# A mixture-of-experts routing stage: weights multiplied by ScalarE, smaller one-hot chunks, experts counted on partitions, and gathers recorded in order

## The chip, the cores and the metric

The kernel runs on one NeuronCore of a Trainium2 chip. Its engines work side by side, each through its own list of instructions in order: PE (TensorE, matrix products; PEld is its weight load), DVE (VectorE), ACT (ScalarE), POOL (GpSimd, which also issues the indirect DMAs) and SP (SyncE, which issues the plain DMAs). They wait for each other through semaphores. SBUF is the working memory, with 128 partitions; PSUM takes what PE computes. The metric is the device time of one execution in microseconds, the median of several runs. All data are float32.

## The reference, cut to what matters

The input is one image of 256 channels and 48x48 pixels, which is 2304 tokens of 256 numbers. Three blocks follow, each added to the stream:

- group norm and an attention of 4 heads in which the 2304 x 4 head rows all attend to each other (9216 queries, 9216 keys);
- layer norm and a "slice" attention: 64 slices, tokens assigned softly by a softmax `sw`, attention among slice tokens, and back to the tokens with the same weights;
- layer norm and a mixture of eight experts.

The last one is where the change lies:

```python
gate_logits = xf @ Wg + bg
top_w, top_i = jax.lax.top_k(gate_logits, TOP_K)      # TOP_K = 2
top_w = jax.nn.softmax(top_w, axis=-1)
w_dense = jnp.sum(jax.nn.one_hot(top_i, E) * top_w[..., None], axis=1)
for e in range(E):                                     # E = 8
    h = jax.nn.gelu(xf @ W1[e] + b1[e], approximate=False)
    out = out + w_dense[:, e:e + 1] * (h @ W2[e] + b2[e])
```

Only two of the eight experts of a token have a weight other than zero, so the kernel computes only those.

## The kernel before, in words

Tokens lie on the partitions in 18 tiles of 128 (`NTT = 18`, `P = 128`). The kernel is one function, `layers`, with five stages in time. First come the loads and projections, then the first attention, which runs from 67 to about 1239 us and is not touched. Then follow three short stages that the change does touch, and the mixture of experts itself. At the end `to_columns` turns the result back to channels and writes it out. A second call of `layers` stands behind a condition for extreme inputs and is not executed here.

**Who sets the order.** The program is written for a tile framework whose scheduler may reorder instructions within an engine's list. Four wrappers made from the class `InOrder` (line 49), called `pe`, `dve`, `act` and `pool`, pin each instruction behind the one recorded just before it on the same engine. Work recorded through `nc.tensor`, `nc.gpsimd` and so on is left to the scheduler. A pinned instruction stays behind its predecessor, but the scheduler may still move an instruction recorded later, without a pin, ahead of both. Since the wrapper issues every wrapped instruction, the profile gives all of them line 57; they are told apart by the names of their tiles. DMAs on SP (`nc.sync`) are not wrapped.

**Back to tokens and layer norm (lines 857 to 905).** For each of the 18 tiles PE makes `py` = the slice attention's output. DVE adds it to the stream `t_sb` for even tiles. For odd tiles PE itself adds `t_sb` through a product with the identity `ident`, and ACT copies the sum out to `t_sb`. DVE takes mean and variance (`bn_stats`, `bn_aggr`), POOL makes 1/sqrt (`rstd_t`) and the negative product with the mean (`shift`). Tiles go in groups of 6, 6, 4 and 2. After each group SP writes the rows of `t_sb` to memory (`t_d`), and the function `normed` lets ACT compute the normalised rows `tn2` (shown by the profile as `tn`) of the group before, one `ACTIVATE` per tile, which SP writes to `tn_d` in memory. There are two `tn2` buffers, so the third group's waits until the first group's write is done.

**Gating and slots (lines 913 to 999).** DVE computes the logits `lg` from what the slice attention already left in the last eight columns of `t_sb`, subtracts the mean part, multiplies by `rstd_t`, and finds the first and the second maximum of each token (`first_max`). ACT computes `e2`, the exponential of their difference; then it loads its table for gelu. Each expert's tokens are put into whole tiles of 128 rows, called slots. There can be at most `NSL` = 43 slots and at least `SURE` = 36. Products with a triangular and a full matrix of ones (`pin`, `pto`) count tokens before each token; two scans make from these the position of each of the 2 x 18 (choice, tile) pairs' tokens: `first_slot` (which slot) and `row` (which row in it).

**One-hot products (lines 1000 to 1055).** For every one of the K = 36 pairs, `in_tile` is 1 in the column of the slot that the token of this partition goes to, and `in_row` is 1 in the column of the row (it is written over the memory of `t_sb`). `what` is `in_tile` times two numbers per token, the token's index plus one and its gate weight (`wk`, flattened `wkf`). The sum over the 36 pairs of the products `in_row`^T `what` on PE gives in PSUM (`pw`) for each slot and row the token (`slot_t`) and its weight (`slot_w`). DVE builds these in chunks of G = 9 pairs: one multiply for `what` (9 x 2 x 43 = 774 elements), one comparison for `in_row` (9 x 128 = 1152), and `in_tile` in two parts of 18 pairs (774). Between the first two chunks `find_experts` counts on one partition, from the running sums `ends`, which expert each slot belongs to (`expert_i`) and how many slots are used (`used_i`). The function `busy` records products whose result is not used: 7 ahead of the one-hot products and 14 behind them, all into a PSUM tile called `spin`.

**The experts (lines 1057 to 1195).** For each slot `rows` (line 1081) gathers 128 rows of `tn_d` by `slot_t` with an indirect DMA of POOL into `xs` (two buffers, and seven separate ones, `late_xs`, for the slots after the 36th). `load_w1` loads the expert's first weights, 1 MB, by SP. `turn` transposes `xs` on PE, `first` makes the hidden layer with 16 products and eight gelus, `second` makes 8 products with the second weights, in the middle of which the next slot's `turn` is recorded. DVE adds the bias and multiplies by `slot_w`, and POOL adds the rows to `t_d` by an indirect DMA (line 1142). In this data 39 slots are used. The gathers and the adding DMAs are issued through `nc.gpsimd`, without a pin: in the list of POOL's instructions the seven late gathers stand third to ninth, and slot 2's gather tenth.

Of the kernel before, what the change touches and what calls it, by code (L numbers as in the profile page):

```python
# [9 lines left out]
FP = mybir.dt.float32  # L10
# [5 lines left out]
P = 128  # L16
# [14 lines left out]
E = 8  # L31
# [31 lines left out]
def layers(  # L63
# [666 lines left out]
    with tc.tile_pool(name="sa", bufs=1) as sa:  # L730
# [126 lines left out]
        def normed(i0, n):  # L857

            tn2 = norm.tile([P, 6, C], FP, name="tn2", tag="tn2")
            for i in range(i0, i0 + n):  # L860
                act.activation(
                    tn2[:, i - i0, :], t_sb[:, i, 0:C], AF.Identity,
                    bias=shift[:, i : i + 1], scale=rstd_t[:, i : i + 1],
                )
            nc.sync.dma_start(
                out=tn_d[i0 * P : (i0 + n) * P, :].rearrange("(i p) c -> p i c", p=P),
                in_=tn2[:, 0:n, :],
            )

        shift = const.tile([P, NTT], FP, name="shift")  # L870
        with tc.tile_pool(name="ps_y0", bufs=7, space=PSUM) as ps_y0, tc.tile_pool(
            name="norm", bufs=2
        ) as norm:
            groups = [(0, 6), (6, 6), (12, 4), (16, 2)]
            for g, (i0, n) in enumerate(groups):
                pys = [ps_y0.tile([P, C + E], FP, name="py", tag="py") for _ in range(n)]
                for k, py in enumerate(pys):
                    j, u = divmod(i0 + k, 2)
                    rows = slice(u * S, (u + 1) * S)
                    pe.matmul(py, swT[rows, j, :], tw[rows, :], start=True, stop=(u == 0))  # L880
                for k in range(1, n, 2):
                    pe.matmul(pys[k], ident, t_sb[:, i0 + k, :], start=False, stop=True)
                for k, py in enumerate(pys):
                    i = i0 + k
                    s6 = small.tile([P, 6], FP, name="s6", tag="s6")
                    if k % 2 == 0:
                        dve.tensor_tensor(t_sb[:, i, :], t_sb[:, i, :], py, ALU.add)
                        dve.bn_stats(s6, t_sb[:, i, 0:C])
                    else:
                        dve.bn_stats(s6, py[:, 0:C])  # L890
                        act.copy(t_sb[:, i, :], py)
                    dve.bn_aggr(stats[:, i, :], s6)
                these = slice(i0, i0 + n)
                ve = small.tile([P, n], FP, name="ve6", tag="ve6")
                dve.tensor_scalar(ve, stats[:, these, 1], 1e-5, None, ALU.add)
                pool.tensor_tensor(rstd_t[:, these], ve, mhalf[:, 0:n], ALU.pow)
                pool.tensor_tensor(shift[:, these], stats[:, these, 0], rstd_t[:, these], ALU.mult)
                pool.tensor_scalar(shift[:, these], shift[:, these], -1.0, None, ALU.mult)
                nc.sync.dma_start(
                    out=t_d[i0 * P : (i0 + n) * P, :].rearrange("(i p) c -> p i c", p=P),  # L900
                    in_=t_sb[:, these, 0:C],
                )
                if g > 0:
                    normed(*groups[g - 1])
            normed(*groups[-1])


    used_i = route.tile([1, 1], mybir.dt.int32, name="used_i")
# [5 lines left out]
    with gating, tc.tile_pool(name="onehot", bufs=1) as oh, tc.tile_pool(  # L914
# [82 lines left out]
        row = gp.tile([P, K], FP, name="row")  # L997
        dve.scalar_tensor_tensor(row, first_slot, -BIG, slot, ALU.add, ALU.subtract)
        in_tile = oh.tile([P, K, NSL], FP, name="in_tile")
        what_flat = oh.tile([P, K * 2 * NSL], FP, name="what")  # L1000
        what = what_flat.rearrange("p (k w n) -> p k w n", k=K, w=2)
        in_row = t_flat[:, 0 : K * P].rearrange("p (k r) -> p k r", r=P)
        pwide = ps_lg.tile([P, P], FP, name="pw")
        pw = pwide[:, 0 : 2 * NSL].rearrange("p (w n) -> p w n", w=2)
        busy(7, spin)
        G = 9
        wkf = wk.rearrange("p k i w -> p (k i) w")

        def find_tile(k, n):
# [2 lines left out]
                in_tile[:, ks, :], bc(first_slot[:, ks], [P, n, NSL]),  # L1012
                at_big.unsqueeze(1).to_broadcast([P, n, NSL]), ALU.is_equal,
            )

        past = gp.tile([1, NSL, E - 1], FP, name="past")

        def find_experts():

            dve.tensor_tensor(  # L1020
                past, bc(steps[0:1, 0:NSL], [1, NSL, E - 1]),
                ends[0:1, 0 : E - 1].unsqueeze(1).to_broadcast([1, NSL, E - 1]), ALU.is_ge,
            )
            ex = gp.tile([1, NSL], FP, name="ex")
            dve.tensor_reduce(ex, past, AX.X, ALU.add)
            dve.tensor_copy(expert_i, ex)
            dve.tensor_copy(used_i, ends[0:1, E - 1 : E])

        for k in range(0, K, G):
            ks = slice(k, k + G)  # L1030
            if k % NTT == 0:
                find_tile(k, NTT)
            dve.tensor_tensor(
                what[:, ks], in_tile[:, ks, :].unsqueeze(2).to_broadcast([P, G, 2, NSL]),
                wkf[:, ks, :].unsqueeze(3).to_broadcast([P, G, 2, NSL]), ALU.mult,
            )
            dve.tensor_tensor(
                in_row[:, ks, :], bc(row[:, ks], [P, G, P]),
                back.unsqueeze(1).to_broadcast([P, G, P]), ALU.is_equal,
            )  # L1040
            if k == 0:
                find_experts()
        for j in range(K):
            n = 2 * NSL if j % G == G - 1 else P
            pe.matmul(
                pwide[:, 0:n], in_row[:, j, :], what_flat[:, j * 2 * NSL : j * 2 * NSL + n],
                start=(j == 0), stop=(j == K - 1),
            )
        busy(14, spin)

        empties = gp.tile([P, NSL], FP, name="empties")
        dve.tensor_scalar(empties, pw[:, 0, :], 0.0, spare, ALU.is_equal, ALU.mult)
# [11 lines left out]
    with tc.tile_pool(name="ps_h", bufs=1, space=PSUM) as ps_h, tc.tile_pool(  # L1064
# [14 lines left out]
        late_xs = iter([fp.tile([P, C], FP, name=f"late_xs{s}") for s in range(SURE, NSL)])  # L1079

        def rows(s, xs):
            nc.gpsimd.indirect_dma_start(  # L1082
                out=xs, out_offset=None, in_=tn_d[:, :],
                in_offset=bass.IndirectOffsetOnAxis(ap=slot_t[:, s : s + 1], axis=0),
                bounds_check=NT + P - 1, oob_is_err=True,
            )
            return xs
# [36 lines left out]
        def second(s, hid, meanwhile):  # L1124

            e = expert_of(s, mybir.EngineType.PE)
            py = next(ring_py)
            for f in range(NHC):
                pe.matmul(
                    py, hid[:, f, :],  # L1130
                    w2_sb[:, bass.ds(e, 1), f, :].rearrange("p e d -> p (e d)"),
                    start=(f == 0), stop=(f == NHC - 1),
                )
                if f == 2:
                    meanwhile()
            e = expert_of(s, mybir.EngineType.DVE)
            y = next(ring_y)
            dve.tensor_tensor(
                y, py, b2_e[:, bass.ds(e, 1), :].rearrange("p e d -> p (e d)"), ALU.add
            )  # L1140
            dve.tensor_scalar(y, y, slot_w[:, s : s + 1], None, ALU.mult)
            nc.gpsimd.indirect_dma_start(  # L1142
                out=t_d[:, :], out_offset=bass.IndirectOffsetOnAxis(ap=slot_t[:, s : s + 1], axis=0),
                in_=y, in_offset=None, bounds_check=NT + P - 1, oob_is_err=True,
                compute_op=ALU.add,
            )
# [128 lines left out]
```

## Time and profile before

| what | us |
|---|---|
| median of 3 runs | 1622.19 (1619.83 to 1622.56) |
| the profiled execution's own time | 1621.32 |
| its span, first to last instruction | 1619.3 |
| PE busy | 1569.0 (97%), 13230 products' passes |
| DVE busy | 1046.2 (65%) |
| ACT busy | 810.8 (50%) |
| POOL busy | 140.3 (9%) |
| mean granted TensorE clock | 0.990 |

The span is made of instructions on the chip; the device time holds a little more before and after them, 2.0 us in this execution. A row of the profile's timeline gives the start in us, the duration, the engine, the source line, the operation, its output and inputs with sizes, and in brackets how long the engine had been idle before it and what ended the wait. In a table of stages each engine has its busy time and, in brackets, its number of instructions; the three last numbers of a row are the granted TensorE clock, the mean busy share of the DMA engines and GB/s. A float32 product shows as two passes of PE, each with its weight load. Durations of single instructions overlap a little where the next does not depend on the one before.

### The profile page before, as it was taken

How to read it: one execution, taken by the hardware profiler on the slowest of the kernel's cores; microseconds unless marked ns; L12 is line 12 of the kernel's file. 1: busy time of each engine (PE TensorE's matmuls, PEld its weight loads, DVE VectorE, ACT ScalarE, POOL GpSimd, SP SyncE). 2: the span in 40 equal slices, each digit the busy share in tenths (PEclk: the TensorE clock that was granted, in tenths of full speed). 3: DMA queues.
4: the chain of work that ended last, by engine and by line, in shares of the span. 5: the costliest groups of instructions: out<-in, count | busy, mean ns of one | idle time of the engine just before them, and what ended most of it. 6: DMA issues, size and time to landing. Idle time of an engine off the chain costs nothing. (4 is left out here: it accounts for less than half of the span.)

```text
span 1619.3 us, 31854 instructions
## 1 busy us (share of the span) xinstructions
PE 1569.0 (97%) x13230; PEld 786.1 (49%) x13230; DVE 1046.2 (65%) x1369; ACT 810.8 (50%) x1100; POOL 140.3 (9%) x128
## 2 busy tenths in 40 slices
PE   7999999999999999999999999999999699999995
PEld 3633343333333333333333333333335489999995
DVE  7577778777787877877878778778687721111111
ACT  2365555555555655556556555565553322333321
POOL 0000000000000000000000000000000143333321
PEclk9999999999999999999999999999999899999997
DMA  4000000000000000000000000000003756666665
GB/s 137 1 1 1 1 1 1 1 1 1 1 1 1 2 1 1 1 1 2 1 1 1 1 1 1 1 1 1 1 2 98 253 182 189 178 181 190 173 157 181
DMA packets 39910, 79.26 MB, mean 49 GB/s; under 512 B 3613, under 2 KB 26218, under 8 KB 39626
## 3 DMA queue, kind: packets, MB, share of 16 engines
q1 hardware_dynamic: 32074, 66.35, 12.3%
q0 software_dynamic: 7680, 10.75, 3.8%
q8 instruction: 108, 1.77, 0.5%
q14 instruction: 48, 0.39, 0.1%
HBM read 64.64 MB, written 12.45 MB: 48 GB/s over the span
## 5 line engine op out<-in xcount | busy, mean ns | idle before, releaser
L57 DVE TENSOR_TENSOR acc<-acc,p 128x1024 f32<-128x1024 f32 x612 | 748.2, 1222 | 251.6 <-ACT p L57 243.5
L57 ACT ACTIVATE p<-s 128x1024 f32<-128x1024 f32 x648 | 662.9, 1023 | 490.0 <-PE s L57 479.8
L57 PE MATMUL av<-p,v_sb 64*64 64x512 f32 x5184 | 675.4, 590 | 1.0 <-DVE up L57 0.7
L57 PE MATMUL s<-q,kk 64*64 64x512 f32 x5184 | 676.2, 591 | 0.0
L57 PEld LDWEIGHTS s<-q,kk 64*64 64x64 f32 x5184 | 201.6, 133 | 352.6 <-issue 181.7
L57 PEld LDWEIGHTS av<-p,v_sb 64*64 64x64 f32 x5184 | 195.6, 131 | 358.3 <-ACT p L57 202.5
L57 ACT ACTIVATE hid<-ph,bcol 128x128 f32<-128x128 f32 x312 | 89.3, 368 | 216.9 <-PE ph L57 216.2
L57 PE MATMUL py<-w_sb,hid 128*128 x624 | 147.3, 379 | 0.0
L57 PEld LDWEIGHTS ph<-xT,w 128*128 128x128 f32 x1248 | 145.3, 192 | 2.7 <-DVE xT L57 0.8
L57 PE MATMUL ph<-xT,w 128*128 128x128 f32 x1248 | 145.7, 275 | 0.5 <-DVE xT L57 0.5
L57 POOL TENSOR_TENSOR rstd_t<-ve,mhalf 128x1 f32<-128x1 f32 (+3 forms) x22 | 28.0, 1271 | 1234.1 <-DVE ve L57 1234.1
L57 DVE COPY xT<-pt 128x256 f32<-128x256 f32 x40 | 17.0, 425 | 173.3 <-PE pt L57 173.3
L57 PEld LDWEIGHTS py<-w_sb,hid 128*128 128x128 f32 x624 | 112.7, 190 | 12.2
L1142 POOL DMA_INDIRECT t_d<-y,slot_t x39 | 61.7, 1583 | 98.7 <-DVE y L57 86.2
L57 DVE TENSOR_TENSOR y<-py,b_bc 128x256 f32<-128x256 f32 x39 | 16.6, 425 | 68.6 <-PE py L57 68.6
L1082 POOL DMA_INDIRECT xs<-tn_d,slot_t x36 | 38.4, 1065 | 110.6 <-PE pt L57 83.8
L57 DVE RECIPROCAL rinv<-pb 128x256 f32<-128x256 f32 x18 | 31.5, 1751 | 0.0
L57 DVE TENSOR_TENSOR acc<-p 128x1024 f32<-128x1024 f32 x18 | 22.1, 1225 | 9.9 <-ACT p L57 9.9
L314 DVE TENSOR_SCALAR q<-pp,bcol 64x512 f32<-64x512 f32 (+1 forms) x30 | 20.8, 694 | 7.4 <-PE pp L297 7.1
L57 DVE TENSOR_REDUCE up<-av 128x512 f32<-128x1024 f32 x18 | 21.9, 1217 | 0.0
L319 ACT ACTIVATE kk<-pp,bcol 128x512 f32<-128x512 f32 (+1 forms) x10 | 6.4, 644 | 21.8 <-PE pp L301 21.8
L297 PE MATMUL pp<-t_sb,WqT 128*128 128x512 f32 (+1 forms) x40 | 17.2, 553 | 0.0
(260 smaller groups left out, 602.0 us busy)
## 6 DMA issues: line engine op xcount, KB each, us to landing
w<-in_L_ffn_W_dram SPq DMA_DIRECT2D x40, 1024.0 KB, 5.6
w_sb<-in_L_ffn_W_dram SPq DMA_DIRECT2D x8, 1024.0 KB, 13.1
x_sb<-in_x_dram SPq DMA_DIRECT2D x4, 576.0 KB
t<-t_d SPq DMA_DIRECT2D x4, 512.0 KB, 6.9
out_dram<-ob SPq DMA_DIRECT2D x4, 512.0 KB
t_d<-t_sb SPq DMA_DIRECT2D x2, 768.0 KB, 3.6
tn_d<-tn SPq DMA_DIRECT2D x2, 768.0 KB, 3.7
b_bc<-in_L_ffn_b_dram SPq DMA_DIRECT2D x1, 1024.0 KB
```

The source lines that it names most:

```text
L57: return self.tc.keep_in_program_order(getattr(self.engine, name)(*args, **kwargs))
L297: nc.tensor.matmul(pq[:, 0:tn], WqT[:, c, cols], xn[:, c, toks], start=(c == 0), stop=(c == 1))
L314: nc.vector.tensor_scalar(dst, pq[rows, 0:tn], bcol[rows, B_Q + m : B_Q + m + 1], 0.125, ALU.add, ALU.mult,)
L319: nc.scalar.activation(kk[:, m, toks], pk[:, 0:tn], AF.Identity, bias=bk_m)
L1082: nc.gpsimd.indirect_dma_start(out=xs, out_offset=None, in_=tn_d[:, :], in_offset=bass.IndirectOffsetOnAxis(ap=slot_t[:, s : s + 1], axis= ...
L1142: nc.gpsimd.indirect_dma_start(out=t_d[:, :], out_offset=bass.IndirectOffsetOnAxis(ap=slot_t[:, s : s + 1], axis=0), in_=y, in_offset=None ...
```

## The change

It has five parts.

1. In the loop over groups PE's products are recorded pair by pair: each odd tile's product with the identity follows its own first product, where before all first products of a group came first.
2. `normed` of the first group is still recorded in the second pass of the loop, those of the other three groups after the loop. In the resulting list of ACT the last copy to `t_sb` stands ahead of the second group's six `tn` activations; in the list of SP the last write to `t_d` stands ahead of that group's write to `tn_d`.
3. The one-hot tiles are built in chunks of 3, 6, 9, 9, 6 and 3 pairs; `in_tile` in parts of 9, 9 and 18. DVE multiplies only the token half of `what`; the weight half is made by ACT, one `ACTIVATE` with `AF.Copy` and a per-partition `scale` for each of the 36 pairs (43 elements). The products are recorded chunk by chunk with the tiles. `find_experts` compares on 128 partitions, one slot on each, sums over seven experts, transposes the column with PE to a row `pex`, and DVE copies this to `expert_i` ahead of the third chunk.
4. Behind the one-hot products stand 9 unused products in place of 14.
5. The gathers and the adding DMAs of the experts are issued through `pool`, with the pin. In the resulting list of POOL five late gathers stand third to seventh, slot 2's gather eighth, the two other late gathers after it; slots 3 and 4 follow as before. Elsewhere in the experts' part, PE's list differs in the first slot alone, where the third product of `second` stands ahead of the second slot's products of `first`, not behind them.

```diff
@@ back to tokens @@
                     pe.matmul(py, swT[rows, j, :], tw[rows, :], start=True, stop=(u == 0))
-                for k in range(1, n, 2):
-                    pe.matmul(pys[k], ident, t_sb[:, i0 + k, :], start=False, stop=True)
+                    if u == 1:
+                        pe.matmul(py, ident, t_sb[:, i0 + k, :], start=False, stop=True)
...
-                if g > 0:
-                    normed(*groups[g - 1])
-            normed(*groups[-1])
+                if g == 1:
+                    normed(*groups[0])
+            for group in groups[1:]:
+                normed(*group)
@@ one-hot products @@
-        what_flat = oh.tile([P, K * 2 * NSL], FP, name="what")
-        what = what_flat.rearrange("p (k w n) -> p k w n", k=K, w=2)
+        what_flat = oh.tile([P, K * 2 * NSL + P], FP, name="what")
+        what = what_flat[:, 0 : K * 2 * NSL].rearrange("p (k w n) -> p k w n", k=K, w=2)
...
             )
-
-        past = gp.tile([1, NSL, E - 1], FP, name="past")
+            for j in range(k, k + n):
+                act.activation(what[:, j, 1], in_tile[:, j, :], AF.Copy, scale=wkf[:, j, 1:2])
 
         def find_experts():
 
+            past = gp.tile([P, E - 1], FP, name="past")
+            dve.tensor_scalar(past, ends[:, 0 : E - 1], token1[:, 0:1], None, ALU.is_lt)
+            ex = gp.tile([P, 1], FP, name="ex")
+            dve.tensor_reduce(ex, past, AX.X, ALU.add)
+            pex = ps_lg.tile([1, P], FP, name="pex")
+            pe.transpose(pex, ex, ident)
+            dve.tensor_copy(used_i, ends[0:1, E - 1 : E])
+            return pex
+
+        find_tile(0, 9)
+        k = 0
+        for n in (3, 6, 9, 9, 6, 3):
+            ks = slice(k, k + n)
+            if k == 9:
+                dve.tensor_copy(expert_i, pex[:, 0:NSL])
+                find_tile(9, 9)
+            elif k == 18:
+                find_tile(18, 18)
+            dve.tensor_tensor(what[:, ks, 0], in_tile[:, ks, :], bc(wkf[:, ks, 0], [P, n, NSL]), ALU.mult)
             dve.tensor_tensor(
-                past, bc(steps[0:1, 0:NSL], [1, NSL, E - 1]),
-                ends[0:1, 0 : E - 1].unsqueeze(1).to_broadcast([1, NSL, E - 1]), ALU.is_ge,
-            )
-            ex = gp.tile([1, NSL], FP, name="ex")
-            dve.tensor_reduce(ex, past, AX.X, ALU.add)
-            dve.tensor_copy(expert_i, ex)
-            dve.tensor_copy(used_i, ends[0:1, E - 1 : E])
-
-        for k in range(0, K, G):
...
+                in_row[:, ks, :], bc(row[:, ks], [P, n, P]),
+                back.unsqueeze(1).to_broadcast([P, n, P]), ALU.is_equal,
             )
             if k == 0:
-                find_experts()
-        for j in range(K):
...
-        busy(14, spin)
+                pex = find_experts()
+            for j in range(k, k + n):
+                cols = P if k + n - j > 1 else 2 * NSL
+                pe.matmul(
+                    pwide[:, 0:cols], in_row[:, j, :], what_flat[:, j * 2 * NSL : j * 2 * NSL + cols],
+                    start=(j == 0), stop=(j == K - 1),
+                )
+            k += n
+        busy(9, spin)
@@ rows, and the adding DMA in second @@
-            nc.gpsimd.indirect_dma_start(
+            pool.indirect_dma_start(
```

More of the change, by code (lines that the diff above doesn't have):

```diff
@@ L1005, in layers @@
         busy(7, spin)
-        G = 9
         wkf = wk.rearrange("p k i w -> p (k i) w")
@@ L1029, in layers @@
-        for k in range(0, K, G):
[L1030 to L1039, printed above, removed]
+            past = gp.tile([P, E - 1], FP, name="past")
@@ L1040, in layers @@
             )
             if k == 0:
-                find_experts()
-        for j in range(K):
[L1044 to L1048, printed above, removed]
-        busy(14, spin)
+                pex = find_experts()
[5 more added lines that the diff above has]
+                )
@@ L1141, in second @@
             dve.tensor_scalar(y, y, slot_w[:, s : s + 1], None, ALU.mult)
-            nc.gpsimd.indirect_dma_start(
+            pool.indirect_dma_start(
                 out=t_d[:, :], out_offset=bass.IndirectOffsetOnAxis(ap=slot_t[:, s : s + 1], axis=0),
```

## The prediction

> **What bounds the kernel now.** The page first: PE is busy 97% of the span, but the chain that ended last reaches back only 30 us, to 1589 us, so neither says what a routing edit is worth. The attention before 1239 us and the output copy are untouched. I cut the stretch from 1262 us into stages (busy us and count of each engine, then PE clock):
>
> ```profile
> 1262.40:1277.60 15.20, 9.60 (x50) 5.52 (x46) 13.63 (x49) 7.33 (x18) 5.05 (x9) 0.92 0.93 321
> 1277.60:1289.10 11.50, 4.43 (x13) 3.81 (x14) 8.43 (x33) 6.52 (x13) 1.16 (x4) 0.51 0.72 240
> 1289.10:1300.90 11.80, 7.93 (x61) 7.12 (x59) 11.64 (x15) 0.00 (x0) 0.00 (x0) 1.00 0.44 172
> 1300.90:1308.90 8.00, 8.00 (x48) 7.27 (x47) 0.76 (x4) 0.00 (x0) 3.35 (x3) 1.00 0.15 45
> 1320.40:1597.00 276.60, 274.48 (x1879) 256.11 (x1879) 47.28 (x122) 84.60 (x296) 95.08 (x71) 1.00 0.63 175
> ```
>
> Those are the rows I read: until 1300.9 DVE is the busiest engine and ACT idles through the third stage; from 1320.4 PE is full (7.25 us per slot), which the change cannot shorten. So all is decided between 1262 and 1320 us, in series. The timeline there:
>
> ```profile
> 1275.92 3.06 ACT L57 ACTIVATE tn<-t_sb,shift,rstd_t 128x256 f32<-128x256 f32 x6
> 1278.88 0.36 ACT L57 COPY t_sb<-py 128x264 f32<-128x264 f32 x1
> 1279.28 0.31 DVE L57 TENSOR_TENSOR lg<-t_sb,lg 128x144 f32<-128x144 f32 x1 [1.36 <-ACT t_sb L57]
> 1283.19 1.09 ACT L57 ACTIVATE tn<-t_sb,shift,rstd_t 128x256 f32<-128x256 f32 x2 [1.80 <-DMA tn_d<-tn]
> ...
> 1298.65 0.96 DVE L57 TENSOR_TENSOR what<-in_tile,wk 128x774 f32<-128x774 f32 x1
> 1298.79 4.38 PE L57 MATMUL pw<-what,t_sb 128*128 128x128 f32 x36 [0.90 <-DVE t_sb L57]
> 1299.53 1.35 DVE L57 TENSOR_TENSOR t_sb<-row,back 128x1152 f32<-128x1152 f32 x1
> 1303.01 6.24 PE L57 MATMUL spin<-Wqkv_sb,ident 128*128 128x256 f32 x28
> 1304.94 1.33 POOL L1082 DMA_INDIRECT xs<-tn_d,slot_t  x1 [25.83 <-DVE slot_w L57]
> ...
> 1309.09 0.38 PE L57 MATMUL pt<-ident,xs 128*128 128x128 f32 x2
> 1317.10 1.01 POOL L1082 DMA_INDIRECT xs<-tn_d,slot_t  x1 [0.30 <-issue]
> 1320.43 0.44 PE L57 MATMUL pt<-ident,xs 128*128 128x128 f32 x2 [1.52 <-DMA xs<-tn_d,slot_t]
> ```
>
> Four losses: a t_sb copy stuck behind six normalisations holds DVE for 1.36 us; PE starts the last 18 one-hot products when the third in_row is written (1298.74) and runs them in 4.3 us; the 14 spins hold the first transpose although its gather (issued 1304.94, 3.1 us to landing by its tile) was there at 1308.04; and PE waits 1.52 us for slot 2's gather, tenth in POOL's queue at 1.32 us a piece.
>
> [...] Here the clock falls to 0.50 inside 1275 to 1276, some 3 us after PE's last work at 1272.7, and is back at about 1288.8, 4.2 us after work resumed.
>
> **The change, part by part**, in the times of the run before.
>
> 1. Products of py in pairs (same 27 matmuls). DVE's second tile waited 0.36 us for its identity product, queued behind six others; six passes of 0.13 us after 1261.56 are over before DVE asks (1263.48). Gain 0.36; from there DVE runs without a gap to 1277.5 before and after.
>
> 2. Normalisation of groups 1 to 3 behind the loop. By the order of instructions the last t_sb copy now stands ahead of the six tn. It is done about 1277.34, so lg's subtraction starts at 1277.6 and its product with rstd_t when POOL has that: 1278.51-0.36+0.03 = 1278.18, against 1279.69. Gain with step 1: 1.51. Late next: those six tn end at 1280.3 instead of 1278.98, so tn_d of group 1 goes out later (t_d of the last group is now ahead of it on SP). Its 768 KB at the 345 GB/s of this stretch land near 1284.0, where the last two tn wait (1283.19 before); they take 1.09, and the exp of e2 queues behind them: e2 at about 1285.4. DVE asks at 1286.87-1.51 = 1285.36. I take 0.2 off (bounds 0 and 0.7). The last tn_d also goes out 0.8 later; its 256 KB are over 1.9 us after the issue, near 1287, and the one-hot tiles, which wait for it, are due at 1287.8. **Front: 1.3.**
>
> 3. One-hot tiles. DVE from 1289.10, durations from the row of 774 (966 ns) and the row of 1152 (1348 ns) cut by length, 80 to 90 ns overlap where the next does not depend: in_tile 387 (0.60), what 129 (0.21), in_row 384 (0.47), past and sum on 128 partitions (0.21, 0.09), used_i (0.06), what 258 (0.35), in_row 768 (0.87), expert_i from PSUM (0.10), in_tile 387 (0.60), what 387 (0.48), in_row 1152 (1.27), in_tile 774 (1.00), what 387 (0.48): 6.79, so the third in_row of nine (the k=18 chunk) starts at 1295.89 and ends at 1297.24 against 1298.74. The 18 products left then run on PE unbroken as before, and the last two DVE chunks (end near 1299.2) are ahead of it. Gain 1.5. The counting of experts alone goes from 1.13 us (four ops, 1292.25 to 1293.38) to about 0.46.
>
> The 36 activations of 128x43 with one pointer, which no row shows: [...] by the nearest rows 218 (128x18, no pointer) to 591 (128x256, two). [...] PE takes the last one at about 1301.3. So they are hidden behind PE up to 0.33 us each; I cost them at nothing. Queued behind them on ACT is only gelu, due after 1310. **One-hot: 1.5.** The extra transpose (0.27 us) on PE falls where PE idled 1.96 us (1290.5 to 1292.4). expert_i on SP comes no later than before.
>
> 4. Nine spins for fourteen. They end 4.0 us after the products instead of 6.2; the gather lands 1.84+3.1 = 4.9 after. PE then follows the landing: 1308.88 (first weight load) to 1308.08. The cover gone, PE idles 0.9 us, well under the 3 us that cost the clock above. **Gain 0.8** (0 to 1.0).
>
> 5. Gathers. The instruction order shows less than the words: five late gathers still stand ahead, but slot 2's is eighth, not tenth: issued 9.53 after the first instead of 12.16. PE reaches it 3.1+9.8 = 12.9 after the first gather (9.8 from the trace, 1309.09 to 1318.92). Landing: late gathers took 2.8 to 5.1 us, the slow ones while a 1 MB w tile passes at 410 GB/s. [...] In that shadow I take 3.3 to 4: 12.8 to 13.5. So of 1.52 us some 0.3 stays. **Gain 1.2** (0.6 to 1.5). Slot 3's gather stays eleventh (6.6 us to landing, lands 20.1 after the first, PE there at about 20.2): nothing, at worst 0.5 lost.
>
> Sum: 1.3+1.5+0.8+1.2 = 4.8 us. The span 1619.3 becomes 1614.5, the profiled execution 1621.3 becomes 1616.5; it lies 0.9 below the median of the three, so the forecast is 1622.19-4.8 = 1617.4.
>
> **Rivals.** (a) The small covers fail: e2 0.7 late, the one-hot tiles 0.3 late for their tn_d, slot 2 back to a 1.1 us wait, slot 3 0.5. Gain 4.8-0.5-0.3-0.8-0.5 = 2.7: 1619.5. For it: margins of 0.1 to 0.8 us; against: they need not all go one way. (b) PE loses its clock in the gap after nine spins and xT's 0.5 us: 4.2 us at half rate cost 2.1: 1619.5. Against: [...] the transpose lies between. (c) Slower: ACT becomes the bound. In the one-hot stage the products would end at 1289.7+36s+0.25 in place of 1303.1; with the other 3.3 us gained, break-even is s = 0.46 us per activation, 0.2% slower at 0.55; at the 591 ns of tn, without overlap, 36x0.591 = 21.3 gives +4.8: 1627.0. [...] (d) The change doesn't do what it says: the order of gathers is a scheduler's, and if slot 2's wait only moves, 3.6 is left: 1618.6.
>
> **How the numbers follow.** Forecast, with (d) as a tenth of all cases inside it: 0.75; (a) 0.14; (b) 0.05; (c) 0.06. A measurement of this kernel can tell about 0.2%, 3.2 us, from no change. The forecast is faster by that bar in about 0.95 of its cases, (a) and (b) in about 0.35: 0.71+0.07 = 0.78 faster; (c) leaves 0.05 slower; 0.17 the same. Range: 2 us below for slot 2's wait, spins and e2 at their good ends plus the spread of the three runs, 3 above to take in (a) and (b): 1615.2 to 1620.4.
>
> **What would show it.** Step 2: no ACT wait on lg, w1st waiting at most 0.3 for e2. Step 3: [...] the last products starting 1.5 us earlier against in_tile. Step 4: the first pt released by its gather, clock 1.00. Step 5: slot 2's pt waiting under 0.5. Wrong if w1st or in_tile waits a microsecond, if pw waits on ACT late in the stage, or if the clock falls before slot 0.

## The result and the profile after

Nine runs of the changed kernel have a median of 1616.83 us (1615.27 to 1618.39), nine of the kernel before beside them 1621.86. The ratio is 0.997, with a 95% interval of 0.9961 to 0.998: faster by 5.0 us, where 4.8 was forecast. The profiled execution is the longest of the nine, 1618.39 us, with a span of 1616.4.

The part ahead of the tokens' stage is the same program in both, yet it took 0.93 us longer in the profiled execution of the changed kernel; over all executions profiled for this study the row that makes `tw` starts anywhere from 1259.72 to 1262.00 us. So every time below is counted from the start of that row (1261.07 before, 1262.00 after). Counted so, the stages up to the first `pt` of two executions agree to some 0.05 us as long as the program up to there is the same. The stages behind it, in which PE waits for transfers, agree less well: slot 2's wait alone is anything from 1.35 to 1.73 us where its gather has the same place.

| from .. to | before | after | change | forecast |
|---|---|---|---|---|
| `tw` .. first `in_tile` | 28.03 | 26.40 | -1.63 | -1.3 |
| `in_tile` .. `empties` (one-hot products done) | 14.11 | 12.54 | -1.57 | -1.5 |
| `empties` .. first `pt` on PE | 5.88 | 4.92 | -0.96 | -0.8 |
| first `pt` .. slot 2's `pt` | 11.34 | 10.67 | -0.67 | -1.2 |
| slot 2's `pt` .. the last slot's | 271.98 | 271.97 | 0.0 | 0 |
| last slot's `pt` .. end of span | 26.89 | 27.90 | +1.0 | 0 |

The four stages that the change touches give 4.83 us. The last row gives 1.0 back, in the loads of `t_d` behind the last adding DMA (4.08 us from the first load's issue to PE before, 5.10 here); in the other thirteen profiles of this study, whatever the kernel, it takes 26.5 to 27.1 us, so this is of the one execution.

The stage table of the changed kernel (stretch, length, busy us and count of PE, PEld, DVE, ACT and POOL, granted PE clock, DMA share, GB/s):

```profile
1262.00:1288.40 26.40, 16.49 (x68) 9.20 (x67) 22.38 (x81) 13.74 (x30) 6.41 (x12) 0.77 0.90 307
1288.40:1300.94 12.54, 11.11 (x81) 10.16 (x80) 9.87 (x21) 8.29 (x36) 0.00 (x0) 0.93 0.45 170
1300.94:1305.86 4.92, 3.88 (x18) 3.06 (x17) 0.76 (x4) 0.00 (x0) 2.59 (x3) 1.00 0.09 28
1323.83:1592.00 268.17, 267.17 (x1830) 249.26 (x1828) 46.03 (x119) 82.24 (x289) 91.53 (x68) 1.00 0.63 175
```

In the second row DVE is busy 9.87 us of 12.54, where it was 11.64 of the first 11.80 us of this stage before, and ACT, idle before, has its 36 activations. The third row holds the gap behind nine unused products: PE is busy 3.88 of 4.92 us and its clock stays at 1.00. The last row is the full PE of the experts, as it was.

The timeline of the changed kernel, the lines that answer to those shown of before (start, duration, engine, line, operation, count, and in brackets the idle time before it and what ended it):

```profile
1277.97 5.02 ACT L57 ACTIVATE tn<-t_sb,shift,rstd_t 128x256 f32<-128x256 f32 x10
1278.47 0.31 DVE L57 TENSOR_TENSOR lg<-t_sb,lg 128x144 f32<-128x144 f32 x1
1278.99 0.31 DVE L57 TENSOR_TENSOR lg<-lg,rstd_t 128x144 f32<-128x144 f32 x1 [0.22 <-POOL rstd_t L57]
1284.87 1.09 ACT L57 ACTIVATE tn<-t_sb,shift,rstd_t 128x256 f32<-128x256 f32 x2 [1.88 <-DMA tn_d<-tn]
1285.87 0.20 ACT L57 ACTIVATE e<-e 128x18 f32<-128x18 f32 x1
1286.17 0.16 DVE L57 TENSOR_SCALAR w1st<-e 128x18 f32<-128x18 f32 x1
...
1294.70 4.09 ACT L57 ACTIVATE what<-in_tile,wk 128x43 f32<-128x43 f32 x18 [0.64 <-DVE in_tile L57]
1295.18 1.35 DVE L57 TENSOR_TENSOR t_sb<-row,back 128x1152 f32<-128x1152 f32 x1
1296.68 4.22 PE L57 MATMUL pw<-what,t_sb 128*128 128x128 f32 x36 [0.53 <-ACT what L57]
1300.73 4.09 PE L57 MATMUL spin<-Wqkv_sb,ident 128*128 128x256 f32 x18
1302.66 1.33 POOL L57 DMA_INDIRECT xs<-tn_d,slot_t  x1 [22.93 <-DVE slot_w L57]
...
1305.86 0.44 PE L57 MATMUL pt<-ident,xs 128*128 128x128 f32 x2 [1.04 <-DMA xs<-tn_d,slot_t]
...
1312.19 1.01 POOL L57 DMA_INDIRECT xs<-tn_d,slot_t  x1 [0.30 <-issue]
...
1316.53 0.44 PE L57 MATMUL pt<-ident,xs 128*128 128x128 f32 x2 [0.78 <-DMA xs<-tn_d,slot_t]
```

`lg` no longer waits 1.36 us for ACT, only 0.22 for POOL. The exponential `e` ends at 1286.07, one tenth ahead of `w1st`, which has no bracket: the later `tn` did queue ahead of it, as feared, and cost nothing. The last 18 one-hot products start when their `in_row` (the row of 1152 elements) is done at 1296.53. The bracket of that line names ACT, but its first weight of the 18 was there at about 1295.03 (1294.70 and 0.33) and the others follow every 0.22 us: of two signals the page names one, and here it is the one that had long come. The first `pt` is released by its gather, and slot 2's still waits for its own, 0.78 us.

### The profile page after: what moved, and what is told of

Its sections match the earlier page's. It is cut to its first block, busy times and chain, and to the rows that moved or that the text cites. A ratio compares the mean times of both kernels' runs of the same rounds, so it can differ in the third digit from the quotient of the medians.

```text
span 1616.4 us, 31879 instructions
## 1 busy us (share of the span) xinstructions
PE 1569.6 (97%) x13221; PEld 785.6 (49%) x13221; DVE 1044.1 (65%) x1374; ACT 818.6 (51%) x1136; POOL 140.5 (9%) x128
```

## The experiments

Each was read in the same stages; a column is the length of one stage in us, the first from the start of `tw`. One profiled execution each:

| kernel | to `in_tile` | to `empties` | to first `pt` | to slot 2's `pt` | place of slot 2's gather |
|---|---|---|---|---|---|
| before | 28.03 | 14.11 | 5.88 | 11.34 | 10th |
| pairs (part 1 alone) | 27.55 | 14.12 | 5.88 | 11.17 | 10th |
| front_only (parts 1 and 2) | 26.41 | 14.13 | 5.87 | 11.56 | 10th |
| onehot (part 3 alone) | 28.03 | 12.53 | 5.88 | 11.48 | 10th |
| spins (part 4 alone) | 28.03 | 14.12 | 4.90 | 10.37 | 7th |
| changed kernel | 26.40 | 12.54 | 4.92 | 10.67 | 8th |
| no_act (changed, weight half by DVE) | 26.40 | 13.69 | 4.85 | 10.36 | 7th |
| spin0 (changed, no unused product) | 26.39 | 12.54 | 4.88 | 13.58 | 9th |
| act15 (changed, 54 activations) | 26.39 | 15.77 | 4.89 | 10.68 | 8th |
| act2 (changed, 72 activations) | 26.40 | 22.57 | 4.88 | 10.69 | 8th |
| again (changed, once more) | 26.40 | 12.53 | 4.92 | 11.87, with a stall | 8th |
| after14 (changed, 14 unused products) | 26.39 | 12.54 | 5.87 | 14.61, with a stall | 10th |
| late (changed, late gathers behind slot 4's) | 26.40 | 12.53 | 4.91 | 9.71 | 3rd |
| spread (changed, late gathers one by one) | 26.43 | 12.54 | 4.87 | 9.71 | 3rd |

### The front: the pairs alone, and with the moved normalisation

The first of these is the kernel before with this edit alone; the second adds the moved calls of `normed`.

```diff
                     pe.matmul(py, swT[rows, j, :], tw[rows, :], start=True, stop=(u == 0))
-                for k in range(1, n, 2):
-                    pe.matmul(pys[k], ident, t_sb[:, i0 + k, :], start=False, stop=True)
+                    if u == 1:
+                        pe.matmul(py, ident, t_sb[:, i0 + k, :], start=False, stop=True)
```

> The kernel before with part 1 alone. Times count from the start of the row that makes tw. Theory (0.36 us from the pairs, the rest from part 2): the second tile's statistics no longer wait 0.36 us for PE, DVE and with it the copies of ACT shift by that much, so lg's subtraction starts at +17.85 in place of +18.21, still behind a wait of about 1.36 us for ACT. Rival: the wait only moves to a later tile or is absorbed by ACT, and lg stays at +18.2. Everything behind lg as before: 9.82 us from lg's subtraction to in_tile, 14.11 from in_tile to empties.

Measured: `lg`'s subtraction at +17.74 and `in_tile` at +27.55, 0.48 us earlier, with the wait for ACT still there:

```profile
1279.53 0.31 DVE L57 TENSOR_TENSOR lg<-t_sb,lg 128x144 f32<-128x144 f32 x1 [1.37 <-ACT t_sb L57]
```

The theory holds, though not its size. Most of what lies between 0.48 and 0.36 has a reason in the trace: two instructions of DVE that don't wait for each other overlap by 0.08 to 0.09 us, and the statistics of the second tile lost this overlap too while they waited.

> The kernel before with parts 1 and 2. Theory: lg's subtraction at +16.5 and in_tile at +26.4, against +18.21 and +28.03 before: 1.6 us, w1st not waiting for the exponential. From in_tile to empties 14.11 us, from there to the first transpose 5.88 and 1.52 us of wait for slot 2, all as before; so slot 2's transpose is 1.6 us earlier. Rival (the covers fail): with the rest of the routing as before, the later write of tn_d or the later exponential makes DVE wait, and in_tile is at most 1.0 earlier.

Measured: `lg` at +16.48, `in_tile` at +26.41, no wait of `w1st`. So the pairs are worth 0.48 us and the moved normalisation 1.14. Slot 2 waited 1.73 us, not 1.52, though nothing behind the routing was changed; the four kernels with that gather in tenth place wait 1.35 to 1.73. The gain at slot 2 is 1.39. This run also warns of single times: it took 1618.73 us, 2.93 less than the run of the kernel before beside it, while the stages account for 1.39. The row `tw` alone starts 1.34 us earlier than in the first profile of before, for no reason that is in the edit.

### The one-hot stage: alone, and without ACT

> The kernel before with part 3 alone, 14 unused products kept. Theory: in_tile at +28.03 as before, from in_tile to empties 12.5 us against 14.11; empties to first transpose 5.9 and slot 2's wait 1.5 as before, since nothing behind the products is changed. Rival: the gain needs the earlier front (tn_d is written later there), and here ACT or PE waits for something else: less than 1 us.

The edit is part 3 of the diff as it stands, in the kernel before. Measured: 12.53 us from `in_tile` to `empties`, and everything ahead of it and up to the first `pt` to 0.01 us as before. Part 3 stands by itself: 1.58 us.

```diff
-            for j in range(k, k + n):
-                act.activation(what[:, j, 1], in_tile[:, j, :], AF.Copy, scale=wkf[:, j, 1:2])
...
-            dve.tensor_tensor(what[:, ks, 0], in_tile[:, ks, :], bc(wkf[:, ks, 0], [P, n, NSL]), ALU.mult)
+            dve.tensor_tensor(
+                what[:, ks], in_tile[:, ks, :].unsqueeze(2).to_broadcast([P, n, 2, NSL]),
+                wkf[:, ks, :].unsqueeze(3).to_broadcast([P, n, 2, NSL]), ALU.mult,
+            )
```

> The changed kernel with the weight half of what made by DVE again, in the same chunks of 3, 6, 9, 9, 6, 3 (one product of 2x43 elements for each pair, no activation). Theory (ACT's help carries the gain): up to the chunk that starts the last 18 products, DVE has 27 x 43 = 1161 elements more at 0.96 per ns, 1.2 us; from in_tile to empties 13.7 us in place of 12.54. Rival (the small chunks and the short counting of experts carry it): at most 0.5 us is lost, 13.0 or less. In this program's list slot 2's gather stands seventh, not eighth, so its wait should be shorter than the 0.78 us of the changed kernel.

Measured: 13.69 us, as expected. The 0.96 elements per ns are those of the changed kernel's profile, where an `in_row` of 384 elements takes 549 ns and one of 1152 takes 1350. The timeline shows where the time goes: the same `in_row` as above is done 1.2 us later against `in_tile` (which is at 1287.62 in this execution), after a product of 774 elements instead of 387 in each of the two large chunks:

```profile
1294.73 0.97 DVE L57 TENSOR_TENSOR what<-in_tile,wk 128x774 f32<-128x774 f32 x1
1295.61 1.35 DVE L57 TENSOR_TENSOR t_sb<-row,back 128x1152 f32<-128x1152 f32 x1
1297.02 4.25 PE L57 MATMUL pw<-what,t_sb 128*128 128x128 f32 x36 [0.90 <-DVE t_sb L57]
```

So of the 1.57 us, ACT's help is 1.15, and the small chunks with the short counting of experts are 0.42; these two were not separated.

### How near ACT is to being the bound

Every second weight activation issued twice (54 in all), and every one (72), the same values written again:

```diff
             for j in range(k, k + n):
                 act.activation(what[:, j, 1], in_tile[:, j, :], AF.Copy, scale=wkf[:, j, 1:2])
+                if j % 2 == 0:
+                    act.activation(what[:, j, 1], in_tile[:, j, :], AF.Copy, scale=wkf[:, j, 1:2])
```

> The changed kernel with every second weight activation issued twice (54 in place of 36, the same values). Theory: at 0.221 us apart this is 0.33 us for each pair, the break-even of the prediction, so from in_tile to empties 12.5 to 12.8 us against 12.54; PE is behind ACT by a hair. Rival (ACT already sets the pace): 18 x 0.22 = 4 us more, about 16.5.

> The changed kernel with every weight activation issued twice (72, the same values). Theory: 0.44 us for each pair makes ACT the bound of this stage: 36 x 0.442 = 15.9 us from the first activation, which starts 0.6 after in_tile, and 0.3 behind it: in_tile to empties 16.8 us against 12.54, PE waiting for what of ACT late in the stage. Rival (ACT is hidden by more than was worked out): under 14 us.

Measured: 15.77 and 22.57 us. Both miss, the first by 3 us, the second by nearly 6. The timeline of the second:

```profile
1288.60 21.16 ACT L57 ACTIVATE what<-in_tile,wk 128x43 f32<-128x43 f32 x72 [1.41 <-DVE in_tile L57]
```

and of the first:

```profile
1288.14 14.62 ACT L57 ACTIVATE what<-in_tile,wk 128x43 f32<-128x43 f32 x54 [1.41 <-DVE in_tile L57]
```

Doubled, an activation and its repetition take 21.16 / 36 = 0.588 us, not 2 x 0.221. Each repetition adds 0.588 - 0.221 = 0.367 us (0.370 with 54), more than an activation's own duration, 0.314 to 0.333 us in this run: the repetition, which writes the same place, does not overlap with the activation ahead of it, while activations of different pairs do, 0.221 us apart. The expectation had used the wrong time for one pair, not the wrong rule. Put in the times that ran, 14.62 / 36 = 0.406 and 0.588 us for each pair, and the rule of rival (c), 36 times this and a nearly fixed rest, gives both: 15.77 - 14.62 = 1.15 and 22.57 - 21.16 = 1.41 us are left for the start and the last products. The longer rest goes with the clock. In the run with 72 activations it falls to 0.50 during this stage, though PE shows as busy for 6.39 of the 7.26 us before:

```profile
1288.01:1295.27 7.26, 6.39 (x29) 4.15 (x27) 7.12 (x16) 6.31 (x23) 0.00 (x0) 0.97 0.30 90
1295.30:1312.30 17.00, 17.00 (x57) 14.51 (x58) 3.46 (x9) 13.64 (x50) 0.00 (x0) 0.50 0.21 87
```

From ACT's last activation to `empties` it is 0.82 us there and 0.55 with 54, where the clock stays at 1.00. Set against the 12.54 us of the changed kernel, ACT becomes the bound at (12.54 - 1.15) / 36 = 0.32 us for each pair (0.31 with the other rest), an estimate from these two runs; the prediction had 0.33. The weights take 0.221, so some 0.1 us of cover is left for each. The time agrees: with 72 activations the kernel takes 1627.03 us against 1623.26 for the kernel before beside it. Rival (c) was a real one: at 0.591 us each it had the products end 8.2 us later than before, and at 0.588 `in_tile` to `empties` is 8.46 longer. Only the 0.221 us that an activation took kept it off.

### The unused products

The kernel before with 9 in place of 14, and the changed kernel with none:

```diff
-        busy(14, spin)
+        busy(9, spin)
```

> The kernel before with part 4 alone: 9 unused products for 14. In the resulting list slot 2's gather already stands seventh, where it was tenth, though the gathers are issued as before. Theory: from empties to the first transpose 4.9 us against 5.88, the clock stays at 1.00; slot 2's gather goes out 7.9 us after the first and lands 4.3 later, before PE asks (13.0 after the first), so its wait of 1.52 us is at most 0.2. Together slot 2's transpose is 2.3 to 2.5 us earlier against in_tile. Rival (the clock): the gap of about 1 us lowers the clock, and the first slot takes 2 us longer. Rival (pinning the gathers is what shortens the wait): slot 2 waits 1.5 us or more.

Measured: first `pt` 4.90 us after `empties`, released by its gather, clock 1.00, and 10.37 us to slot 2's `pt`, which waits 0.48. Both stages together are 1.95 us shorter (2.3 to 2.5 expected), a miss: the gather landed 5.3 us after its issue, not 4.3. This edit alone moves slot 2's gather from tenth to seventh place, through `nc.gpsimd` and with no pin. The lists of instructions complete the point: the kernel before with the `pool` wrapper alone has the same lists on all five engines as the kernel before, and the changed kernel without it the same as the changed kernel. Part 5 changes nothing. How the scheduler comes to its order was not looked into; the place follows no simple rule (with 14, 9 and no unused products in the changed kernel it is tenth, eighth and ninth).

> The changed kernel with no unused product behind the one-hot products (slot 2's gather ninth in its list). PE has nothing to do for some 5 us until the first gather lands. Theory: the first transpose stands as in the changed kernel (4.92 us after empties), but the clock falls to about half and stays there some 4 us, so that from the first transpose to slot 2's it takes 12 to 13 us against 10.67. Rival (the unused products do nothing for the time): the clock stays at 1.00 and that stretch takes 10.7 to 11.5, the upper end for the later gather.

Measured: first `pt` where it was, then 13.58 us to slot 2's in place of 10.67. The stages of that kernel around the silence and behind it:

```profile
1300.65:1305.53 4.88, 0.00 (x0) 0.00 (x1) 0.76 (x4) 0.00 (x0) 2.55 (x3) 1.00 0.10 29
1307.50:1308.50 1.00, 1.00 (x7) 1.00 (x7) 0.00 (x0) 0.00 (x0) 0.70 (x2) 0.50 0.22 53
1311.50:1312.50 1.00, 1.00 (x6) 1.00 (x6) 0.00 (x0) 0.06 (x1) 0.69 (x2) 0.50 0.34 66
```

PE is silent for 4.9 us; the clock is at 0.50 from 1305.7, just after the work came back, to 1312.5, and slot 0 takes 2.9 us longer. From the first product on the half clock lasted 7 us here, and 4.2 in the kernel before. The fall comes 5.1 us after PE's last product here, and 2.45 in the kernel before (1272.74 to 1275.19), where the prediction has some 3; a gap of 1.96 us there, in the one-hot stage (up to 1292.43), left the clock at 1.00. The traces show a grid behind this. Apart from the first and the last of a profile, every stretch of one clock in the profiles of before and after is a whole number of times 3.41 us long: 13.65 in the kernel before, from 1275.19 to 1288.84, and 13.65 in the changed kernel, from 1276.47 to 1290.12. Here it is 6.83, from 1305.72 to 1312.54. In all three the clock comes back at the end of the first step of 3.41 us in which PE is busy throughout (from 1309.13 here, from 1285.43 before, from 1286.71 in the changed kernel); in the step ahead of it PE is busy for 0.85, 0.22 and 0.80 of the time. So in these three the time at half went with where the work fell in the steps; what sets the steps is not shown. Nine products are enough in this place, then, and none is not: the gap in front of the gather is 1.04 us with nine, and no clock is lost.

### The gathers

In the two kernels that follow slot 2's gather is third in POOL's list. In the first, the seven late gathers read their indices from a copy of their columns of `slot_t`, made in slot 3's pass:

```diff
+        slot_l = fp.tile([P, NSL - SURE], FP if slot_t.dtype == FP else slot_t.dtype, name="slot_l")
         def rows(s, xs):
+            at = slot_t[:, s : s + 1] if s < SURE else slot_l[:, s - SURE : s - SURE + 1]
...
-                in_offset=bass.IndirectOffsetOnAxis(ap=slot_t[:, s : s + 1], axis=0),
+                in_offset=bass.IndirectOffsetOnAxis(ap=at, axis=0),
...
+            if s == 3:
+                dve.tensor_copy(slot_l, slot_t[:, SURE:NSL])
```

In the second, each late gather has a copy of its own, made just ahead of it, so that the late gathers come one by one in the middle of the experts:

```diff
         def rows(s, xs):
+            at = slot_t[:, s : s + 1]
+            if s >= SURE:
+                at = fp.tile([P, 1], slot_t.dtype, name=f"slot_l{s}")
+                dve.tensor_copy(at, slot_t[:, s : s + 1])
```

The first ran on one chip beside the changed kernel itself and the changed kernel with 14 unused products.

> The changed kernel itself, beside the next two on the same chip: 0.997 of the time before, 1616.8 us. Its profile tells whether the 1 us that the first one lost behind slot 2, in the last adding DMA and the loads behind it, is of the program (then from slot 2's transpose to the end it is 299.9 us again) or of the single execution (298.9 as before).

> The changed kernel in which the seven late gathers read their indices from a copy of the last seven columns of slot_t, which DVE makes in slot 3's pass: in the resulting list slot 2's gather stands third and slots 3 and 4 next, the late ones behind slot 4's. Theory: the 0.78 us of wait for slot 2 are gone, PE is full from the first transpose on, slot 2's transpose comes 9.9 us after the first in place of 10.67, and the median is 0.8 us under the changed kernel's. Rival (the wait moves): the late gathers now delay the steady gathers or adding DMAs, and slots 5 to 9 wait, so the end doesn't move.

> The changed kernel with 14 unused products in place of 9, gathers still pinned. In its list slot 2's gather is tenth again. Theory: empties to the first transpose 5.9 us (4.92), slot 2's wait 1.5 us (0.78), median 1.7 us over the changed kernel's: part 5 is worth nothing, and its gain belongs to part 4. Rival: the pinned gathers shorten the wait by themselves, to 0.8 us.

Measured: the changed kernel 1618.47 us (0.996 of the kernel before, 0.9946 to 0.9973), the late gathers 1617.79 (0.9952, 0.9939 to 0.9966), 14 products 1621.42 (0.9975, 0.9965 to 0.9986). All are slower than expected and so is the kernel before, 1625.5 there. The order is as the theory has it, but the intervals overlap.

The profiles show why these runs say less than hoped: each of the three has one stall of 1.7 to 3 us that no other profile here has. In the one with 14 products it lies behind slot 1's transpose:

```profile
1310.77 0.38 PE L57 MATMUL pt<-ident,xs 128*128 128x128 f32 x2
...
1314.97 1.14 ACT L57 ACTIVATE hid<-ph,bcol 128x128 f32<-128x128 f32 x4 [4.65 <-remote]
1315.02 0.43 DVE L57 COPY xT<-pt 128x256 f32<-128x256 f32 x1 [7.97 <-remote]
1315.49 0.71 PE L57 MATMUL ph<-xT,w 128*128 128x128 f32 x4 [3.05 <-issue]
```

The copy of `pt`, elsewhere 0.4 us behind it, comes 4.2 us behind, and ACT starts again in the same moment. Behind this stall the clock is at 0.50 from 1316.8 to 1320.2. Slot 2's wait can therefore not be read in this run nor in the repeated changed kernel (a stall of about 1.7 us, same place); in the kernel with the late gathers one slot in the middle takes 9.07 us, not 7.14. All three stalls fall into a burst of gathers on POOL, but most bursts pass without one, so a link is only a guess. What can be read: with 14 products, 5.87 us to the first `pt`, the gap as before, and its slot 2's gather is tenth though it is pinned; with the late gathers, 9.71 us from the first to slot 2's `pt` and no wait. From the last slot's `pt` to the end of the span the repeated changed kernel takes 26.96 us: the 1 us lost there in the first profile is not of the program.

> The changed kernel in which each of the seven late gathers reads its indices from a column of its own, copied by DVE just ahead of it: in the resulting list slot 2's gather stands third and the late ones stand one by one between the adding DMAs of the middle slots, with no burst. Theory: slot 2's transpose comes 9.7 us after the first, as with the burst behind slot 4, every later distance between transposes is 7.25 us, so that slot 2's to the last is 271.98 us, and the end is 0.8 to 1.0 us earlier than the changed kernel's: a ratio to the kernel before near 0.9963 where the changed kernel had 0.997 and 0.996. Rival (the seven late gathers only bring their cost to the middle of the experts): single distances over 7.25 there, and slot 2's transpose to the last is over 272.5 us.

Measured: 1614.66 us (1614.5 to 1615.76), the kernel before beside it 1621.96: a ratio of 0.9954 (0.994 to 0.9968). The timeline:

```profile
1305.25 0.44 PE L57 MATMUL pt<-ident,xs 128*128 128x128 f32 x2 [0.99 <-DMA xs<-tn_d,slot_t]
...
1305.96 1.01 POOL L57 DMA_INDIRECT xs<-tn_d,slot_t  x1 [1.21 <-PE pt L57]
...
1310.07 5.46 SPq L1101 DMA_DIRECT2D w<-in_L_ffn_W_dram  x2
...
1314.96 0.38 PE L57 MATMUL pt<-ident,xs 128*128 128x128 f32 x2
```

Slot 2's gather now goes out as soon as its buffer is free, 4.1 us ahead of the first load of `w` that follows, and slot 2's transpose waits for nothing. From it to the last slot's it is 271.9 us, so the late gathers cost nothing where they are now. This version beats the kernel before, and by its profile the changed kernel too, by 0.96 us at slot 2; by the times alone its interval still overlaps that of the changed kernel.

**What slot 2's wait hangs on.** The runs with different places of that gather show more than the order. A 1 MB load of `w` goes out 0.2 us after slot 1's transpose. The rows of the kernel with 9 products alone:

```profile
1311.60 5.03 SPq L1092 DMA_DIRECT2D w<-in_L_ffn_W_dram  x2
...
1311.81 1.01 POOL L1082 DMA_INDIRECT xs<-tn_d,slot_t  x1 [0.31 <-PE pt L57]
...
1317.14 0.44 PE L57 MATMUL pt<-ident,xs 128*128 128x128 f32 x2 [0.48 <-DMA xs<-tn_d,slot_t]
```

| place of slot 2's gather | issued after the `w` load | taken by PE after the `w` load | issue to use |
|---|---|---|---|
| 10th (before, pairs, front_only, onehot) | 3.23 to 3.24 | 6.41 to 6.79 | 3.2 to 3.6 |
| 8th (changed kernel, act15, act2) | 1.50 to 1.56 | 5.84 to 5.87 | 4.3 |
| 7th (spins, no_act) | 0.21 to 0.27 | 5.54 | 5.3 |
| 9th (spin0) | 0.07 ahead of it | 5.82 | 5.9 |
| 3rd (spread) | 4.1 ahead of it | no wait | - |

Issued 3 us earlier within the load, the gather is there only 0.9 to 1.3 us earlier. Issued 0.07 us ahead of the load, it is used 5.82 us behind the load's start, which is no gain either. Wherever it went out with the load in these runs, it landed behind the load. Counted from the load's issue, the load lands after 5.1 us and the gather after 5.5 with 9 products alone; in the kernel before, after 5.4 and 6.5; in the changed kernel, after 5.1 and 5.8. In the kernel with 9 products the 16 DMA engines are busy for 0.82 of the time from 1313 to 1315 us and for 0.99 from 1315 to 1317, and what they move is at first nearly all the load's. From 1313 to 1316 us the queue of the plain loads (q1) moves 0.97 MB and that of the gathers (q0) 0.02 MB, though slot 2's gather was issued at 1311.81; in the next us q0 moves 0.36 MB:

```profile
q1 hardware_dynamic: 242, 0.97, 85.6%
q0 software_dynamic: 6, 0.02, 2.0%
...
q0 software_dynamic: 127, 0.36, 91.5%
```

A row has the packets, the MB and the share of the 16 engines' time. Why the gathers' packets come last there is not shown.

## Why the prediction was right, step by step

- **Steps 1 and 2, the front: 1.3 forecast, 1.63 measured.** The pairs gave 0.48, not 0.36; with part 2, `lg`'s product with `rstd_t` came 1.63 earlier, not 1.51. The 0.2 taken off for the exponential was not needed. Its working was right to 0.3 us: the exponential forecast at 1285.4 in the times of before, found at 1285.14, and DVE asking at 1285.36, found at 1285.24. The cover was real but thin, 0.1 us.
- **Step 3, one-hot: 1.5 forecast, 1.57 measured.** The sum of DVE's rows held. That the activations would cost less than the 0.33 us that PE hides (5.9 us, from 1295.4 to 1301.3, for 18) was the author's estimate, which no row of before shows. Nine took 2.10 us, the first 0.33, so they are 0.221 apart and hidden, with the edge at about 0.32 us. They brought no table load: `ACT_TABLE_LOAD` (1.28 us each) stands twice in both profiles, the second time in that of the changed kernel at 1286.09, ahead of all 36.
- **Step 4, nine products: 0.8 forecast, 0.96 measured.** The forecast set the landing against the first weight load, 0.2 us ahead of the first product; against the product it is 1.0. The gather takes over as the releaser and the clock stays at 1.00, so rival (b) is refuted for a gap of 1 us; where the gap was 4.9 us the clock did fall, and slot 0 took 2.9 us longer, not 2.1.
- **Step 5, gathers: 1.2 forecast, 0.67 measured.** This is the step that failed, in two ways. The term mis-sized is the landing "in that shadow": 3.3 to 4 us were taken and 4.3 ran, since the gather landed behind the whole load (0.7 us after it), so 0.78 of the wait was left and not 0.3. Counting 1.32 us for each place in POOL's queue was right for the issue and wrong for the landing. And the gain was put down to the pinned gathers; the lists and the run with nine products show that it belongs to part 4, and that part 5 does nothing. Rival (d) was right that the order is the scheduler's, and wrong that the wait would only move.
- **Rival (a)** did not come: no cover failed but part of slot 2's, and slot 3 took 7.30 us after slot 2 as it did before (7.31).

The misses have opposite signs, 0.33 and 0.07 and 0.16 up and 0.53 down, which is why 4.83 came so near to 4.8; that nearness is luck. The three larger terms, over 4 us of it, were each within 0.35 and each was shown by itself.

## What to carry to other kernels

Count stages from an instruction that stands in both programs just ahead of the change: read so, edits of 0.5 us are plain in single executions whose whole times scatter by 3. Here a transfer that was late behind a queue of issues was not won back place by place while a large load was under way: 3 us in the issue gave 0.9 to 1.3 at the use, and the wait was gone when it went out 4.1 us ahead of the load. Look for such a load first, and move the transfer ahead of it by giving the transfers in its way something real to wait for. And compare the instruction lists before crediting an edit: here the pin that was to order the gathers changed no list, while five unused products fewer did.

## What had not been expected of the hardware

- After a silence of 4.9 us TensorE's clock stayed at half for some 7 us of work; after the silence of 11.9 us in the routing of the kernel before it was 4.2. Between its first and its last change in the profiles of before and after the clock keeps one value for whole multiples of 3.41 us, and it also fell where PE shows as busy for 6.39 of 7.26 us (72 activations).
- In the three runs made side by side, each profile held a stall of 1.7 to 3 us. In the one with 14 products ACT, SP and DVE start again at 1314.97, 1314.97 and 1315.02, in the one with the late gathers SP, DVE and ACT at 1347.91, 1347.95 and 1347.99. The kernel before took 1625.5 us beside them; on the same chip a single execution at another time took 1621.66. The cause stays open.
- A gather of 128 rows that goes out with a 1 MB load came 5.5 us after the load's start when issued 0.2 us behind it, and 6.4 to 6.8 when issued 3.2 behind it; while the load ran in the kernel with 9 products alone, the gathers' queue moved 0.02 MB in 3 us.
